# A third weights buffer, hats asked for in every pass, products spread over two passes, and smaller buffers elsewhere, in a deformable-convolution block

## The chip, the cores and the metric

One NeuronCore of a Trainium2 chip runs the whole program. The metric is device time in microseconds (us) of one execution. Executions of one kernel lie within about 0.5% of each other. Every kernel was timed in rounds with the kernel before on the same chip. A ratio is the mean time of one kernel's fast runs over that of the kernel before's fast runs of the same rounds, so it is not quite the ratio of the medians that are quoted; it comes with a 95% interval.

## The reference, cut to what matters

The input is (2, 256, 128, 128) in f32. Layer 0 normalises it, then runs three branches of deformable depthwise convolution with dilations 1, 9 and 12; each branch samples 9 taps at positions moved by learned offsets, with bilinear weights:

```python
py = yy - pad + ky * dil + off[:, :, 0]
px = xx - pad + kx * dil + off[:, :, 1]
sampled = _bilinear(x, py, px)              # four neighbours, weight (1-|dy|)(1-|dx|)
y = einsum('bckhw,ck->bchw', sampled, wk)   # 9 taps, per channel
x_i = gelu(ln2d(y))
# out = ln2d(x1 + x2 + x3 + conv1x1(x)); h = mlp(out); x = x + ln2d(h + out)
```

Layer 1 is a 3x3 convolution with ternary weights. The change does not touch it.

## The kernel before

There are three stages: A makes the normalised image as a table in DRAM and, for every tap, *hats*, the one-dimensional weights max(0, 1-|offset - r|) (negated) for rows and for columns; B samples; C is layer 1. The change is in B.

B works in units: one image, one row of tiles (3 rows high), one branch. A tile `xs` is a patch of 9 x 14 pixels (126 partitions) by 256 channels; 17 tiles make a row of tiles, and all three branches use them. For a unit, the matrix `A` (126 x 3456) holds the bilinear weights. It is the product of the column hats, which are loaded straight into `A`, and the row hats `hy`, which VectorE multiplies in, one product for each `ky` (three a unit inside the image). TensorE multiplies every tile by its part of `A` into PSUM (`pm`), ScalarE copies `pm` to `ev`, and VectorE adds the taps of `ev` into a ring of output rows (the *sums*). A unit has two passes, one for each half of the channels. Between these matmuls a *tail* is woven in, one step at a time: norms, GELU, the 1x1 convolution and the MLP of finished rows.

```python
def load_columns(u):                 # SyncE's queue, straight into A
    for ky in taps(u):
        src, at, n = hat_rows(u, ky, TR, [[HY * 3 * W, TC], [0, TR]])
        pin(nc.sync.dma_start(k["A"][u % 2][0:PT, AO + at : AO + at + n], src))

def load_rows():                     # ScalarE's queue, into one of HBUFS = 3 tiles
    if ahead and len(hys) < HBUFS:
        ...
        pin(nc.scalar.dma_start(hy[0:PT, 0:n], src))

def build():                         # the product
    hy, u, at, n = hys.popleft()
    A = k["A"][u % 2][0:PT, AO + at : AO + at + n]
    pin(nc.vector.tensor_tensor(A, A, hy[0:PT, 0:n], ALU.mult))

def sample(u, c):                    # one pass
    for T in range(0, NT, 2):
        # two tiles: matmuls into pm, one copy pm -> ev; in the last pass of a row also
        # load_tile(next row, T + XAHEAD); XAHEAD = 4
        for _ in range(-(-len(pending) * 2 // (NT + 1 - T))):
            pending.popleft()()      # sums of the pass before, products
        if c == 0 and T == 0:
            for _ in range(HBUFS): load_rows()
        tail.advance()
    ...                              # cut: the first XAHEAD tiles of the next row
    if kys: pending.extend(sums(u, c, ev))
    if c == KC - 1:
        if u + 2 < len(units): load_columns(u + 2)
        pending.append(lambda: complete(u))
    elif u + 1 < len(units):
        pending.extendleft([build] * len(taps(u + 1)))   # all products of u+1 first
```

`pin` keeps the emitted order, so the order in which these calls are made is the order on every engine.

## Time and profile before

| | kernel before |
|---|---|
| median of the first 3 runs | 8623.69 us (8601.57 to 8631.41) |
| profiled span | 8590.6 us |
| first to last pm matmul | 957 to 7303 us, 264 units, 24.04 us each |
| granted TensorE clock in that stage (share of full speed) | 0.91 |
| VectorE idle in front of the products | 1061.8 us |
| ScalarE waiting for the sums to free `ev` | 869.3 us |

The group line of the products shows how such a line is read: line, engine, operation, names, shapes, count; then busy us and mean ns of one; then the idle time in front of them with what ended it.

```profile
L727 DVE TENSOR_TENSOR A<-A,hy 126x1152 f32<-126x1152 f32 (+2 forms) x752 | 1000.7, 1344 | 1061.8 <-DMA hy<-hats 618.6 <-DMA A<-hats 361.9 <-PE pm L826 39.7
```

VectorE stands as long before the 752 products as it works on them. Both factors come late: the row hats (618.6 us) and the columns (361.9 us).

### The profile page before, as it was taken

How to read it: one execution, taken by the hardware profiler on the slowest of the kernel's cores; microseconds unless marked ns; L12 is line 12 of the kernel's file. 1: busy time of each engine (PE TensorE's matmuls, PEld its weight loads, DVE VectorE, ACT ScalarE, POOL GpSimd, SP SyncE). 2: the span in 40 equal slices, each digit the busy share in tenths (PEclk: the TensorE clock that was granted, in tenths of full speed). 3: DMA queues.
4: the chain of work that ended last, by engine and by line, in shares of the span. 5: the costliest groups of instructions: out<-in, count | busy, mean ns of one | idle time of the engine just before them, and what ended most of it. 6: DMA issues, size and time to landing. Idle time of an engine off the chain costs nothing. (4 is left out here: it accounts for less than half of the span.)

```text
span 8590.6 us, 100764 instructions
## 1 busy us (share of the span) xinstructions
PE 7303.7 (85%) x33648; PEld 5392.7 (63%) x33648; DVE 6012.3 (70%) x11183; ACT 4362.5 (51%) x8530; POOL 1160.6 (14%) x1740
## 2 busy tenths in 40 slices
PE   6999778888888888888887888888888888789999
PEld 3555576766666766776666766766766766334444
DVE  7666467777767777776667777767777776387676
ACT  2444345655555655555655655555655556433232
POOL 0000001211211211112211111211221112200000
PEclk9999788999899989999989998999999999799999
DMA  8777566666666666665566666666666665212121
GB/s 298 197 192 197 171 200 209 213 195 213 206 191 201 211 200 201 217 204 185 187 190 211 217 200 215 204 196 199 217 203 192 217 206 174 86 69 77 66 78 53
DMA packets 776262, 1579.90 MB, mean 184 GB/s; under 512 B 96496, under 2 KB 492232, under 8 KB 771376
## 3 DMA queue, kind: packets, MB, share of 16 engines
q1 hardware_dynamic: 588528, 872.06, 32.9%
q10 hardware_dynamic: 122688, 466.35, 16.6%
q0 software_dynamic: 64512, 234.91, 8.2%
q8 instruction: 270, 4.42, 0.2%
q14 instruction: 264, 2.16, 0.1%
HBM read 1306.71 MB, written 266.36 MB: 183 GB/s over the span
## 5 line engine op out<-in xcount | busy, mean ns | idle before, releaser
L826 PE MATMUL pm<-A,xs 126*128 126x216 f32 (+2 forms) x17952 | 3828.1, 363 | 710.5 <-ACT ev L835 466.3
L826 PEld LDWEIGHTS pm<-A,xs 126*128 126x128 f32 x17952 | 3380.8, 206 | 1183.9 <-ACT ev L835 585.0
L835 ACT COPY ev<-pm 128x432 f32<-128x432 f32 (+2 forms) x4752 | 2202.8, 490 | 2124.0 <-PE pm L826 964.9
L778 DVE SCALAR_TENSOR_TENSOR ring<-ev,defw,ring 128x384 f32<-128x384 f32 (+5 forms) x4376 | 2380.9, 566 | 119.6 <-ACT ev L835 27.5
L727 DVE TENSOR_TENSOR A<-A,hy 126x1152 f32<-126x1152 f32 (+2 forms) x752 | 1000.7, 1344 | 1061.8 <-DMA hy<-hats 618.6
L502 ACT ACTIVATE T<-T,rs 128x256 f32<-128x256 f32 x1280 | 703.5, 606 | 45.3 <-DMA hy<-hats 30.0
L771 DVE TENSOR_SCALAR ring<-ev,defw 128x384 f32<-128x384 f32 (+2 forms) x568 | 308.3, 550 | 471.3 <-ACT ev L835 470.7
L453 PE MATMUL hp<-T,w 128*128 128x512 f32 x1024 | 530.0, 642 | 121.1 <-ACT T L597 116.0
L493 POOL TENSOR_SCALAR rs<-mv 128x4 f32<-128x4 f32 x320 | 181.2, 566 | 3035.5 <-DVE mv L491 2813.8
L1159 PE MATMUL pc<-cring,signs 128*128 128x512 bf16 x2304 | 519.8, 384 | 57.2 <-DVE signs L1047 42.7
L517 PE MATMUL zc<-ident,T 128*128 128x128 f32 x2560 | 405.5, 296 | 169.2 <-DVE T L656 77.1
L1159 PE MATMUL pc<-cring,sums 128*128 128x512 bf16 x2304 | 510.3, 380 | 0.0
L453 PE MATMUL h<-hT,w 128*128 128x512 f32 x1024 | 480.0, 592 | 0.9 <-ACT hT L612 0.9
L517 PEld LDWEIGHTS zc<-ident,T 128*128 128x128 f32 x2560 | 329.5, 152 | 227.1 <-ACT T L502 89.0
L204 PE MATMUL pz<-wz,xa 128*128 128x486 f32 x1024 | 460.5, 582 | 1.5 <-DVE zr L211 1.5
L489 DVE BATCH_NORM_STATS2 st<-T 128x6 f32<-128x256 f32 x1280 | 447.8, 411 | 13.7 <-ACT T L479 13.4
L479 ACT COPY T<-tp 128x512 f32<-128x512 f32 x640 | 384.0, 602 | 144.5 <-DMA hy<-hats 47.5
L1159 PEld LDWEIGHTS <-signs 128*128 128x128 bf16 x2304 | 226.6, 99 | 339.6 <-issue 42.1
L1159 PEld LDWEIGHTS <-sums 128*128 128x128 bf16 x2304 | 225.4, 98 | 274.4 <-DVE sums L1219 0.2
L453 PEld LDWEIGHTS hp<-T,w 128*128 128x128 f32 x1024 | 196.6, 202 | 289.3 <-ACT T L597 167.7
L495 POOL TENSOR_TENSOR rs<-rs,mhalf 128x4 f32<-128x4 f32 x320 | 375.4, 1173 | 0.0
L540 ACT ACTIVATE T<-zc,bb,bw 128x512 f32<-128x512 f32 x384 | 304.0, 794 | 107.1 <-DMA hy<-hats 46.5
(124 smaller groups left out, 6163.7 us busy)
## 6 DMA issues: line engine op xcount, KB each, us to landing
hy<-hats ACTq DMA_DIRECT2D x736, 567.0 KB
A<-hats SPq DMA_DIRECT2D x736, 567.0 KB
xs<-table SPq DMA_DIRECT2D x1496, 126.0 KB
g12d<-T POOLq DMA_DIRECT2D x128, 512.0 KB, 4.9
other<-g12d POOLq DMA_DIRECT2D x128, 512.0 KB, 5.3
hats<-hb SPq DMA_DIRECT2D x192, 240.0 KB
hats<-hb SPq DMA_DIRECT2D x192, 192.0 KB
xl<-x1d SPq DMA_DIRECT2D x56, 640.0 KB
```

The costliest lines, as they stand in the source:

```text
L204: nc.tensor.matmul(pz[:, 0:NZ], lhsT=xt[:, c, r, :], rhs=k["wz"][:, c, :], start=c == 0, stop=c == KC - 1,)
L453: nc.tensor.matmul(out, lhsT=w, rhs=v, start=start and i == 0, stop=stop and i == n - 1)
L479: nc.scalar.copy(Tv[:, 2 * h : 2 * h + 2, :].rearrange("p j c -> p (j c)"), tp)
L489: pin(nc.vector.bn_stats(st[:, j, :], Tv[:, j, :]))
L495: pin(nc.gpsimd.tensor_tensor(rs[:, 0, :], rs[:, 0, :], mhalf[:, 0:NB4], ALU.pow))
L502: nc.scalar.activation(Tv[:, j, :], Tv[:, j, :], AF.Identity, scale=rs[:, 0, j : j + 1], bias=rs[:, 1, j : j + 1],)
L517: nc.tensor.transpose(zc[:, j * P : (j + 1) * P], Tv[:, j, c * P : (c + 1) * P], ident)
L727: pin(nc.vector.tensor_tensor(A, A, hy[0:PT, 0:n], ALU.mult))
L778: nc.vector.scalar_tensor_tensor(dst, src, w, dst, ALU.mult, ALU.add)
L826: nc.tensor.matmul(pm[:, j, 0:n], lhsT=xts[b, Rt][T + j][0:PT, c * P : (c + 1) * P], rhs=rhs, start=True, stop=True,)
L835: nc.scalar.copy(ev[:, q0 * 3 : q1 * 3, T * CI : (T + nt) * CI].rearrange("p m (t j) -> p t m j", j=CI), pm[:, 0:nt, 0:n].rearrange("p t ( ...
L1159: nc.tensor.matmul(pc[:, bank, :], lhsT=w[:, m * P : (m + 1) * P], rhs=xc[:, i, k, t * JC : (t + 1) * JC, kx : kx + W], start=j == 0, stop ...
```

## The change

The intent is to take the products off the critical path: a third `A`, so that products are made ahead of their use, and products spread over both passes instead of standing in a block at the head of one. On-chip memory for the third `A` (13.9 KB a partition) is found by cutting other buffers. One more row of tiles covers the last image rows when the rows are no multiple of three.

```diff
-NORMS = 4
-VBUFS = 9
-HBUFS = 3
-XAHEAD = 4
+NORMS = 3
+VBUFS = 8
+HBUFS = 2
+ABUFS = 3
...
-    NR = (H + 2 * REACH) // RI
+    NR = -(-(H + 2 * REACH) // RI)
...
             while self.norms == NORMS:
-                yield 1, None, 1
+                yield 0                      # and advance() goes on to the next chain
...
-            xt = pool.tile([P, C], F32, name="xs", tag="xs", bufs=NT + XAHEAD)
+            xt = pool.tile([P, C], F32, name="xs", tag="xs", bufs=NT)
...
-                if c == 0 and T == 0:
-                    for _ in range(HBUFS):
-                        load_rows()
+                if T == 0:
+                    load_rows()              # now fills up to HBUFS, ahead of the pops
...
-            if c == KC - 1:
-                if u + 2 < len(units):
-                    load_columns(u + 2)
-                pending.append(lambda: complete(u))
-            elif u + 1 < len(units):
-                pending.extendleft([build] * len(taps(u + 1)))
+            n = [len(taps(v)) if v < len(units) else 0 for v in (u + 2, u + 3)]
+            if c == 0:
+                for i in range(n[0] - 1):
+                    pending.insert(1 + len(pending) * i // 2, build)
+            else:
+                if n[1]:
+                    load_columns(u + 3)
+                    pending.append(build)
+                pending.append(lambda: complete(u))
```

More of the change, by code (lines that the diff above doesn't have):

```diff
@@ L426, in advance @@
                     step = next(item[1], None)
+                    if step == 0:
+                        continue
                     if step is None:
@@ L711, in load_columns @@
                 src, at, n = hat_rows(u, ky, TR, [[HY * 3 * W, TC], [0, TR]])
-                pin(nc.sync.dma_start(k["A"][u % 2][0:PT, AO + at : AO + at + n], src))
+                pin(nc.sync.dma_start(k["A"][u % ABUFS][0:PT, AO + at : AO + at + n], src))
         def load_rows():
-            if ahead and len(hys) < HBUFS:
+            while ahead and len(hys) < HBUFS:
                 u, ky = ahead.popleft()
@@ L725, in build @@
             hy, u, at, n = hys.popleft()
-            A = k["A"][u % 2][0:PT, AO + at : AO + at + n]
+            A = k["A"][u % ABUFS][0:PT, AO + at : AO + at + n]
             pin(nc.vector.tensor_tensor(A, A, hy[0:PT, 0:n], ALU.mult))
@@ L806, in sample @@
             if kys:
-                A = k["A"][u % 2]
+                A = k["A"][u % ABUFS]
                 q0, q1 = (kys[0] + 1) * RI, (kys[-1] + 2) * RI
@@ L843, in sample @@
                     for i in range(T, T + nt):
-                        if i + XAHEAD < NT:
-                            load_tile(*following, i + XAHEAD)
+                        load_tile(*following, i)
+                if T == 0:
+                    load_rows()
                 for _ in range(-(-len(pending) * 2 // (NT + 1 - T))):
                     pending.popleft()()
-                if c == 0 and T == 0:
-                    for _ in range(HBUFS):
-                        load_rows()
                 tail.advance()
@@ L854, in sample @@
                 pending.popleft()()
-            if br == BRS[-1] and c == 0 and u + 1 < len(units):
-                for T in range(XAHEAD):
-                    load_tile(*units[u + 1][0:2], T)
             if kys:
                 pending.extend(sums(u, c, ev))
-            if c == KC - 1:
-                if u + 2 < len(units):
-                    load_columns(u + 2)
+            n = [len(taps(v)) if v < len(units) else 0 for v in (u + 2, u + 3)]
[6 more added lines that the diff above has]
+                    pending.append(build)
                 pending.append(lambda: complete(u))
-            elif u + 1 < len(units):
-                pending.extendleft([build] * len(taps(u + 1)))
         pending = deque()
@@ L870, in sample_near @@
         ahead = deque((u, ky) for u in range(len(units)) for ky in taps(u))
-        for u in range(2):
+        for u in range(ABUFS):
             load_columns(u)
-        for _ in taps(0):
-            load_rows()
-            build()
-        for _ in range(HBUFS):
-            load_rows()
+        for u in range(ABUFS - 1):
+            for _ in taps(u):
+                load_rows()
+                build()
+        load_rows()
+        if taps(ABUFS - 1):
+            pending.append(build)
         for u in range(len(units)):
@@ L986, in conv_preact_kernel @@
             k = {
-                "A": [pool.tile([P, AO + 9 * RI * W + AE], F32, name=f"A{i}") for i in range(2)],
+                "A": [pool.tile([P, AO + 9 * RI * W + AE], F32, name=f"A{i}") for i in range(ABUFS)],
             }
```

## The prediction

> **What bounds the kernel now.** I read the page first, then the busy time by stage, the list of waits, and last the order in time of one stretch. The page says that no engine is full, that TensorE comes nearest, and that its clock is below full in the long middle part only.
>
> ```profile
> PE 7303.7 (85%) x33648; PEld 5392.7 (63%) x33648; DVE 6012.3 (70%) x11183; ACT 4362.5 (51%) x8530; POOL 1160.6 (14%) x1740
> ...
> PEclk9999788999899989999989998999999999799999
> DMA  8777566666666666665566666666666665212121
> ```
>
> The sampling stage runs from the first pm matmul (957 us) to the last (7303 us). The change touches nothing else but an order here and there. The windows give, after the stretch: busy us of PE, PEld, DVE, ACT, POOL, then granted clock, DMA share, GB/s.
>
> ```profile
> 0.00:957.00 957.00, 832.64 (x3401) 466.41 (x3401) 622.61 (x1345) 346.73 (x641) 3.44 (x9) 0.97 0.75 217
> 957.00:7303.00 6346.00, 5307.23 (x25157) 4392.56 (x25158) 4538.74 (x8705) 3599.54 (x7524) 1106.28 (x1635) 0.91 0.63 202
> 7303.00:7600.00 297.00, 200.14 (x662) 99.64 (x662) 151.78 (x345) 124.84 (x189) 50.18 (x95) 0.78 0.23 79
> 7600.00:8590.00 990.00, 963.71 (x4432) 434.11 (x4430) 699.17 (x790) 291.43 (x177) 0.74 (x1) 0.99 0.19 69
> ```
>
> The stage has 2 images x 44 rows of tiles x 3 branches = 264 units, so 6346/264 = 24.04 us a unit, in two passes (one per half of the channels). The waits inside the stage (us in total, times, longest):
>
> ```profile
> ACT ev L835 <- DVE ring L778: 869.3, 169, 12.4
> DVE A L727 <- DMA hy<-hats: 618.6, 303, 8.0
> DVE ring L771 <- ACT ev L835: 470.7, 113, 11.3
> DVE A L727 <- DMA A<-hats: 349.2, 126, 14.7
> ...
> PE pm L826 <- ACT ev L835: 466.3, 250, 6.0
> PE pm L826 <- DVE A L727: 197.2, 57, 29.3
> ```
>
> Read from the bottom: PE waits for ACT to empty pm; ACT waits because the ev buffer it wants (two of them) has not been summed by VectorE; VectorE is late because, ahead of the sums, it stands at the products A = A*hy (L727), whose two factors are still in flight. One instance, VectorE then TensorE:
>
> ```profile
> 3076.20 1.36 DVE L727 TENSOR_TENSOR A<-A,hy 126x1152 f32<-126x1152 f32 x1 [6.19 <-DMA hy<-hats]
> 3078.91 1.36 DVE L727 TENSOR_TENSOR A<-A,hy 126x1152 f32<-126x1152 f32 x1 [1.35 <-DMA hy<-hats]
> 3081.48 1.36 DVE L727 TENSOR_TENSOR A<-A,hy 126x1152 f32<-126x1152 f32 x1 [1.21 <-DMA hy<-hats]
> 3089.00 0.61 DVE L771 TENSOR_SCALAR ring<-ev,defw 128x384 f32<-128x384 f32 x1 [6.16 <-ACT ev L835]
> ```
> ```profile
> 3072.31 3.66 PE L453 MATMUL hp<-T,w 128*128 128x512 f32 x4 [7.16 <-ACT T L597]
> 3075.80 0.90 PE L826 MATMUL pm<-A,xs 126*128 126x216 f32 x4
> 3076.53 1.88 PE L453 MATMUL hp<-T,w 128*128 128x512 f32 x4
> ```
>
> The same four matmuls take 3.66 us just after the 7.16 us gap and 1.88 us four microseconds later: a gap is paid twice, as idle time and as slow matmuls.
>
> **What the Trainium skill says.** The page "TensorE: Matmul & The Clock Gate", Part 1 (the HAM clock gate), says that the array falls to half clock after about 3.4 us of idleness and needs about as long of activity to come back; the trace agrees (granted clock 0.54 from 3072.3 to 3076.0 us, 1.00 after). The same page, under the architectural detail, says ScalarE and VectorE take their queues strictly in order: so a product that waits for a transfer holds up every sum behind it, as above. "DMA: Bandwidth & Descriptors", section "Issuing engines are not separate DMA queues", says transfers started from several engines share the same 16 DMA engines: so asking for hats on ScalarE's queue and columns on SyncE's at once makes both late. "Perfetto Trace Analysis", section "Identifying the Most-Contended Engine", says that a repeating bubble on the engine that should be full can mean too few buffers; here the repeating bubble is at L727 and the A buffers are two.
>
> **What the floors are.** TensorE at full clock: 34 pm matmuls of 216 columns took 6.37 us together (0.187 each); by columns 15640 x 0.187 + 1904 x 0.125 + 408 x 0.062 = 3190 us. The 2360 wide tail matmuls in the stage start 0.43 us apart (3076.53 to 3078.25 for four), 1015 us; the 4848 transposes 0.11 apart, 530 us. Sum 4735 us or 17.9 us a unit. The stage is then 4735 of warm work, 5307 - 4735 = 572 lost to the clock (9% of 6346 is 571), and 6346 - 5307 = 1039 idle. VectorE: 4539/264 = 17.2 us a unit. DMA: 202 GB/s x 6346 us/264 = 4.86 MB a unit; its bursts run at 255 to 290 GB/s, so about 18 us. Three resources of nearly one size, chained by small buffers: none can be filled wholly.
>
> **The change part by part.**
>
> Balance. VectorE's sums are (2378 + 308)/528 = 5.1 us a pass, the three products 1000/264 = 3.8 us a unit, the tail's share 853/528 = 1.6 us a pass. Before, all three products open pass 1: 10.5 us of work there, against 6.7 in pass 0 and 9.0 us of TensorE per pass. So pass 1 is VectorE's even with no wait, and with two ev buffers it cannot lend to pass 0. After, one product closes pass 0 and two lie in pass 1: 8.0 and 9.2 us. That alone is worth at most 10.5 - 9.2 = 1.3 us a unit.
>
> Transfers. Before, at a unit's start three columns and three hats (6 x 0.567 MB) plus the tail's 0.45 MB, nearly 3.9 MB, or 14 us at 270 GB/s, are wanted at the front of pass 1, some 12 us later. VectorE's idle time in front of L727 is 1049 us in all, 4.0 us a unit. After, with a third A, the columns are for the unit three ahead, the first product comes at the end of the next pass, the third in the middle of the one after, and one hat is asked for a pass later. 2.8 MB (10.5 us) are wanted over 11 to 16 us. I expect about three quarters of those 4.0 us to go, and the 197 us of PE waiting straight for A.
>
> What is taken away to pay for it: hats buffers 3 to 2, tail tiles 9 to 8, norms 4 to 3, tiles read ahead 4 to 0. I counted the emitted order: there is no point, before or after, where the sums must push the tail to free a ring; waiting chains average 0.38 before and 0.36 after. So the smaller tail costs nothing in the steady state. The rows of the image that are now read only in the last pass still have a pass to land.
>
> The extra row. Six more units: two are empty, four have one tap (72 columns). Eight passes of 34 narrow matmuls, nine copies of about 0.35 us and a few sums: about 4 us each, +32 us. But they carry tail work: the emitted drain after the last sample shrinks from 277 steps to 231. It took about 200 us, so 46 x 0.72 = -33 us. One more unit prepared at the start: +8 us. About +10 in sum, nothing much.
>
> Sum. TensorE's side: of 24.04 - 17.9 = 6.1 us of idle and slow time a unit I keep 60%, 3.7, since gaps shorten and the clock recovers with them: 21.6. VectorE's side, as a check: 17.2 work + 1.0 left at L727 + the 2.9 of other waits it has now = 21.1. I take the worse: 264 x (24.04 - 21.6) = 644 us gained, 10 lost: 8624 - 634 = 7990. I round up to 8010, for coupling I can't see.
>
> **The rivals.**
>
> (a) The hats become the wait. With two buffers the third hat can't be asked for until the unit's first product is done, at the end of pass 0, and it is ScalarE that stands at the issue, in order, with the pm copies behind it. If the first product waits for its columns, ScalarE stops and TensorE soon after; and the third product follows the issue by only some 5 to 8 us. For it: a hat took long to land in bursts (the 6.19 us above), and ScalarE already shows small waits of this kind (99.5 us before ev). Against it: at that point in pass 1 only tile rows load, and in every third unit alone. If so, half the gain: 8300.
>
> (b) The DMA engines bind at 18 us a unit: waits at L727 stay because supply, not timing, is short. For it: share 0.85 to 0.97 in bursts. Against: whole 5 us stretches near 3085 and 3118 us show under 40 GB/s, so there is room. 8200.
>
> (c) It goes better: TensorE stays warm through the stage and the unit comes to 20.3 us: 7650. Against it: a third of PE's waits is at the tail's matmuls (T, xn), which the change leaves.
>
> (d) No gain, because the copies of ScalarE and the two ev buffers pace it in any case: ACT has 13.6 us a unit of work, so it could not on its own. 8550.
>
> **Range and chances.** A unit between 20.8 and 22.9 us gives 7790 to 8340; I take 7790 to 8370. Everything removed lies on the chain that stops TensorE, and what is added cancels, so faster by over 2% (under 8451) is 0.90, within 2% 0.08, slower 0.02.
>
> **What would show it.** Right: idle time before the products well under 1049 us, say 250 to 450; ACT's wait for the sums of 869 us under half; no PE wait for A; stage clock 0.94 or more; about 21.6 us a unit over 264 full-size units; stages before and after unchanged. Wrong: a large wait of VectorE or ScalarE for hy (rival a), or DMA share near 0.8 with L727 still waiting (rival b).

## The result, and the profile after

The changed kernel takes 8502.81 us (median of 4, 8491.07 to 8530.18) against 8614.66 us of the kernel before in the same rounds: ratio 0.9874, interval 0.9843 to 0.9905. It is 1.3% faster, where 7% was predicted. The prediction was wrong.

The page of the changed kernel:

```profile
PE 7301.8 (86%) x33920; PEld 5371.4 (63%) x33920; DVE 5994.7 (71%) x11212; ACT 4358.4 (51%) x8602; POOL 1144.7 (13%) x1740
...
PEclk9999789999999999999899999999999999899999
DMA  9777667666666666665567666766666665212121
```

The stretches of the sampling stage and of the drain behind it (after: two lines; then the drain of the kernel before):

```profile
947.00:7254.00 6307.00, 5352.75 (x25539) 4396.13 (x25539) 4530.66 (x8774) 3619.30 (x7636) 1101.40 (x1656) 0.92 0.66 205
7254.00:7394.00 140.00, 111.23 (x368) 57.70 (x366) 56.00 (x149) 76.47 (x134) 37.59 (x73) 0.89 0.21 68
```
```profile
7303.00:7499.00 196.00, 152.73 (x477) 80.19 (x476) 68.82 (x191) 99.64 (x174) 48.85 (x93) 0.82 0.20 67
```

The sampling stage lost only 39 us (6346 to 6307) and its clock went from 0.91 to 0.92. More than half of the gain of the profiled runs (8590.6 - 8489.2 = 101 us) is in the drain, from the last pm matmul to the last statistics of the tail, 196 to 140 us. The waits inside the stage (us in total, times, longest):

```profile
DVE A L729 <- DMA hy<-hats: 555.3, 240, 7.6
DVE A L729 <- DMA A<-hats: 424.0, 121, 11.8
ACT ev L837 <- DVE ring L780: 589.2, 180, 8.5
ACT ev L837 <- DVE ring L773: 168.4, 55, 7.2
PE pm L828 <- ACT ev L837: 523.3, 308, 6.6
PE pm L828 <- DMA xs<-table: 152.8, 127, 4.8
PE pm L828 <- DVE A L729: 27.8, 1, 27.8
```
```profile
PE pm L826 <- DMA xs<-table: 24.8, 15, 5.2
```

The last line is of the kernel before. TensorE no longer waits for `A` (197.2 us before; the 27.8 us left are one wait at the start), which is what a third buffer is for. But the products still wait for both factors, 979 us against 968 before, and a new wait has appeared: TensorE for its tiles, 152.8 us against 24.8. ScalarE's wait for the sums stands in two lines now, 757.6 us together, against 869.3 in one line before.

One instance in order of time, from the queues of SyncE and ScalarE and from VectorE:

```profile
3004.38 2.53 SPq L714 DMA_DIRECT2D A<-hats  x3
```
```profile
3008.84 1.68 ACTq L722 DMA_DIRECT2D hy<-hats  x2
```
```profile
3019.05 1.36 DVE L729 TENSOR_TENSOR A<-A,hy 126x1152 f32<-126x1152 f32 x1 [5.00 <-DMA hy<-hats]
```

The columns are asked for at the end of a unit, the hats at the head of the next pass, and the product stands at the end of that pass. So everything lies within one pass, as it did before the change. The product is for a unit that will need it only two units later, and yet VectorE stands 5.00 us for it, with the sums behind it.

### The profile page after: what moved, and what is told of

It reads as the page before. It is cut to its first block, busy times and chain, and to the rows that moved or that the text cites. A ratio compares the mean times of both kernels' runs of the same rounds, so it can differ in the third digit from the quotient of the medians.

```text
span 8489.2 us, 101867 instructions
## 1 busy us (share of the span) xinstructions
PE 7301.8 (86%) x33920; PEld 5371.4 (63%) x33920; DVE 5994.7 (71%) x11212; ACT 4358.4 (51%) x8602; POOL 1144.7 (13%) x1740
## 5 line engine op out<-in xcount | busy, mean ns | idle before, releaser
L828 PE MATMUL pm<-A,xs 126*128 126x216 f32 (+2 forms) x18224 | 3861.7, 360 | 708.9 <-ACT ev L837 523.3
L837 ACT COPY ev<-pm 128x432 f32<-128x432 f32 (+3 forms) x4824 | 2203.8, 488 | 2139.4 <-PE pm L828 1113.3
L729 DVE TENSOR_TENSOR A<-A,hy 126x1152 f32<-126x1152 f32 (+2 forms) x756 | 1015.9, 1344 | 1143.0 <-DMA hy<-hats 555.3
L1146 ACT CAST cring<-D 128x2048 bf16<-128x2048 f32 x128 | 243.3, 1901 | 223.5 <-PE pc L1162 152.7
```

The lines of the kernel that those rows point to most:

```text
L828: nc.tensor.matmul(pm[:, j, 0:n], lhsT=xts[b, Rt][T + j][0:PT, c * P : (c + 1) * P], rhs=rhs, start=True, stop=True,)
L837: nc.scalar.copy(ev[:, q0 * 3 : q1 * 3, T * CI : (T + nt) * CI].rearrange("p m (t j) -> p t m j", j=CI), pm[:, 0:nt, 0:n].rearrange("p t ( ...
```

## The experiments

Three theories stood at first. *L, the lead*: the third buffer's time went between product and use, not between fetch and product. *S, the supply*: the DMA engines cannot deliver faster. *C, the coupling*: the waits of the products are not what a unit's time hangs on.

### e1_late: products one pass later

```diff
             if c == 0:
-                for i in range(n[0] - 1): pending.insert(1 + len(pending) * i // 2, build)
+                if n[0]: pending.append(build)
             else:
-                if n[1]: load_columns(u + 3); pending.append(build)
+                for i in range(n[0] - 1): pending.insert(1 + len(pending) * i // 2, build)
+                if n[1]: load_columns(u + 3)
```

> The changed kernel with each unit's first product moved one pass later and the other two likewise: columns now have two passes from the request to the first product instead of one. Theory L (the third buffer's time went between product and use, not between fetch and product, so the lead of the fetch stayed one pass): VectorE's idle time in front of the products falls from 1143 us to 300 to 500 us, ScalarE's wait for the sums (589 + 168 us) to under 400, time 8200 to 8350 us. Theory S (the DMA engines' supply): idle time moves to the hats, stays over 800 us, time within 0.5% of the change, 8460 to 8540. Theory C (the products' waits are not what the unit's time hangs on): the idle time falls but the time stays within 0.5%.

Measured: 8624.43 us, ratio 1.0006 (0.9979 to 1.0034). It is slower than the change.

```profile
L729 DVE TENSOR_TENSOR A<-A,hy 126x1152 f32<-126x1152 f32 (+2 forms) x756 | 1014.6, 1342 | 1024.2 <-DMA hy<-hats 953.6 <-DMA xs<-table 26.8 <-PE pm L828 16.2
```

The columns' wait is gone from the first three releasers, as L says, but nearly all of it has moved to the hats, 953.6 us. With two hats buffers and three products a unit, the third hat can be asked for only when the first product is done, at the head of the pass in which it is used; and in this version the new columns are asked for at just that time. So L alone falls, and S is not shown either. This is theory H.

### e2_no_columns and e2_no_hats: take the transfers away

Their outputs are wrong, which doesn't matter for the times.

```diff
-            for ky in taps(u):
+            for ky in taps(u) if u < ABUFS else ():       # both: columns of the first units only
...
-            pin(nc.vector.tensor_tensor(A, A, hy[0:PT, 0:n], ALU.mult))
+            pin(nc.vector.tensor_tensor(A, hy[0:PT, 0:n], hy[0:PT, 0:n], ALU.mult))
...                                                        # e2_no_hats: two hats loaded once, kept
```

> Wrong result on purpose: no column loads after the first three units, product = hat times hat. 1.7 of 4.9 MB a unit and every wait for columns are gone. Theory L and theory S both: VectorE's idle time at the products under 400 us and the time 8000 to 8250 us. Theory C: 8400 or more.

> Wrong result on purpose: neither columns nor hats are loaded after the start, product = a kept hat times itself; the products stay. 3.4 of 4.9 MB a unit are gone, no product waits for a transfer. It is the ceiling of what any fetch order could bring. By the prediction's step (products' waits are worth most of 4.0 us a unit): a unit of about 21.6 us, 7850 to 8000 us. Theory C: 8300 us or more, because TensorE, ScalarE and VectorE wait for each other anyway.

Measured: without columns 8150.95 us, ratio 0.9457 (0.9432 to 0.9482); without columns and hats 7687.57 us, ratio 0.8921 (0.8899 to 0.8943). The sampling stage of the second:

```profile
964.00:6467.00 5503.00, 5062.42 (x25538) 4211.75 (x25538) 4493.71 (x8774) 3639.40 (x7636) 1146.84 (x1656) 0.97 0.25 77
```

With the same instructions on VectorE and no product waiting, the stage takes 5503 us, or 20.8 us for each of 264 full units, at clock 0.97. The run also takes the traffic off everything else, so it is a ceiling, and what the waits alone are worth is not shown by it; for that see e6, which keeps the traffic. In e2_no_columns the hats' wait is 283.8 us instead of 555.3, with the hats asked for at the same places: without the columns they come earlier, in part perhaps because the first product, which frees a hats buffer, no longer waits for its columns.

### e3_row and e4_tail: the small parts alone, on the kernel before

```diff
-    NR = (H + 2 * REACH) // RI
+    NR = -(-(H + 2 * REACH) // RI)               # e3_row
```
```diff
-NORMS = 4                                         # e4_tail
-VBUFS = 9
+NORMS = 3
+VBUFS = 8                                         # and yield 0 with its two lines in advance()
```

> The kernel before with nothing but the extra row of tiles. The prediction: +32 us of narrow passes, -33 us of drain, so within 20 us of the kernel before (8600 to 8635). A rival: the row costs 60 us or more and eats the gain of the other parts, 8670 or more.

> The kernel before with nothing but the smaller tail (8 tiles, 3 norms, a chain that waits for a norm no longer takes the step). The prediction: no cost in the steady state, so within 0.4% of the kernel before, 8580 to 8640. Rival: the tail's order is worth part of the 1.3% gained: under 8560.

Measured: e3_row 8617.12 us, ratio 1.0008 (0.9973 to 1.0043); e4_tail 8628.53 us, ratio 1.0012 (0.9980 to 1.0043). On the kernel before neither costs or gains anything that shows.

### e5_hats3 and e6_late_hats3: three hats buffers

```diff
-HBUFS = 2
+HBUFS = 3
-VBUFS = 8
+VBUFS = 7        # room; two constants are moved out of the stage as well
                  # e6: and the products one pass later, as in e1_late
```

> The changed kernel with three hats buffers again (room: tail tiles 8 to 7, and two constants moved out of the stage). Theory H (with two hats buffers each unit's third hat can be asked for only at the start of the pass that uses it, behind the columns): the hats part of VectorE's idle time at the products (555 us) falls under 250, the columns part (424 us) stays, time 8300 to 8420. Theory S (supply of the DMA engines): the sum of both parts stays over 850 us and the time within 0.5% of the change.

> Later products and three hats buffers together: columns have two passes, every hat at least one. Theory H plus L: idle time at the products under 300 us in all (after: 1143, later products alone: 1003), the unit near 22.5 us, time 7950 to 8200. Theory S: idle time over 700 us, 8400 or more. Either alone is known or runs beside it; if this gains more than the sum of the two, each hides the other.

Measured: e5 8433.80 us, ratio 0.9790 (0.9754 to 0.9826); e6 8199.28 us, ratio 0.9510 (0.9478 to 0.9541). Their products, e5 then e6:

```profile
L733 DVE TENSOR_TENSOR A<-A,hy 126x1152 f32<-126x1152 f32 (+2 forms) x756 | 1014.1, 1341 | 751.8 <-DMA A<-hats 609.7 <-DMA hy<-hats 70.1 <-PE pm L832 49.6
```
```profile
L733 DVE TENSOR_TENSOR A<-A,hy 126x1152 f32<-126x1152 f32 (+2 forms) x756 | 1012.4, 1339 | 33.6 <-DMA A<-hats 15.5 <-issue 11.4 <-DMA hy<-hats 6.4
```

Three hats alone take the hats' wait from 555 to 70 us, and the columns' wait grows to 610. Three hats and later products together leave 33.6 us of 1143. So S falls for the waits at the products: the same bytes arrive in time when they are asked for early enough. H and L are both true, and each hides the other. With two hats, later products cost 1.3% (1.0006/0.9874); with three they gain 2.9% (0.9510/0.9790 = 0.9714). With the waits goes time, so C falls too, in its strict form.

The tail of seven tiles needs a control, on the change:

> The change with seven tail tiles instead of eight and nothing else: control for e5, e6, e12. The emitted order has no forced step and a drain of 263 steps instead of 231, so within 0.5% of the change, 8480 to 8550.

Measured: e9_tail7 (only `VBUFS = 7`) 8558.86 us, ratio 0.9958 (0.9924 to 0.9993). That is 0.9% slower than the change, a little more than expected: e5 and e6 gained in spite of their tail, and their true distance from the change is larger by about that much. Against this control e6 is 4.5% faster (0.9510/0.9958), for 1135 us less of waits at the products (1168.4 in e9). That is some 385 us, so a microsecond of these waits was worth about a third of a microsecond of time (an estimate; e6 has other waits that e9 has not).

### e8_spread: the spreading alone, with two A buffers

```diff
 # on the kernel before; A, hats, tail, read-ahead untouched
-            if c == KC - 1:
-                if u + 2 < len(units): load_columns(u + 2)
-                pending.append(lambda: complete(u))
-            elif u + 1 < len(units):
-                pending.extendleft([build] * len(taps(u + 1)))
+            n = [len(taps(v)) if v < len(units) else 0 for v in (u + 1, u + 2)]
+            if c == 0:
+                for i in range(n[0] - 1): pending.insert(1 + len(pending) * i // 2, build)
+            else:
+                if n[1]: load_columns(u + 2); pending.append(build)
+                pending.append(lambda: complete(u))
 # and the hats asked for at the head of every pass, as in the change
```

> The kernel before (two A buffers, three hats, larger tail) with nothing but the products spread over the passes as in the change. The lead of the columns is then the same as in the change. Theory L/H: the third A buffer bought nothing, so this is as fast as the change or a little faster, 8400 to 8530. Rival: the third buffer is what gained the 1.3%, and this stays at 8600 or, with PE waiting for A, is slower.

Measured: 8157.07 us, ratio 0.9464 (0.9433 to 0.9496). This part alone is four times as good as the whole change, and far better than I expected.

```profile
L727 DVE TENSOR_TENSOR A<-A,hy 126x1152 f32<-126x1152 f32 (+2 forms) x752 | 1008.8, 1341 | 482.0 <-DMA A<-hats 380.7 <-DMA hy<-hats 70.5 <-PE pm L826 29.9
...
ACT ev L835 <- DVE ring L778: 509.5, 171, 8.8
ACT ev L835 <- DVE ring L771: 74.7, 37, 5.2
```

Products that are spread wait 482 us instead of 1062, and ScalarE waits 584 us for the sums (two lines) instead of 869.3. No third buffer was needed. (With the products the requests for hats have moved, to the head of every pass; no run separates the two.) So the question turned round: what did the rest of the change take away?

### e10, e11, e14: the cuts, put back onto e8 one by one

```diff
-XAHEAD = 4        # e10_spread_noahead, e14_spread_both_cut
+XAHEAD = 0
-HBUFS = 3         # e11_spread_hats2, e14_spread_both_cut
+HBUFS = 2
```

> The fast e8_spread (two A buffers, three hats, products spread) with the read-ahead of tiles taken away (4 to 0), as the change did. Theory X: SyncE issues a tile every 0.88 us, so 17 of them take 15 us, longer than the pass they are squeezed into, and the columns queue behind them; then the time goes from 8157 to 8380 to 8460, and PE's waits for tiles from 52 us to over 150. Rival: the read-ahead is worth under 0.7%, 8140 to 8215.

> e8_spread with two hats buffers instead of three. Theory H: hats become the wait again (70 us now, 400 or more then), 8230 to 8350. If both cuts add up to what the change lost (8503 - 8157 = 346 us), the third A buffer is worth nothing by itself.

> e8_spread with both cuts of the change at once: two hats buffers and no read-ahead, still two A buffers. If the third A buffer is worth nothing by itself: 8440 to 8520, as the change (8503). If it gains: 8560 or more here. If it costs (its columns, earlier, crowd the hats): 8430 or less.

Measured: e10 8351.33 us, ratio 0.9707 (0.9691 to 0.9723); e11 8272.51 us, ratio 0.9618 (0.9602 to 0.9634); e14 8415.20 us, ratio 0.9785 (0.9751 to 0.9819). The waits, e10, then e11, then e14:

```profile
DVE A L727 <- DMA A<-hats: 578.7, 144, 13.2
...
PE pm L826 <- DMA xs<-table: 168.5, 132, 4.6
```
```profile
DVE A L727 <- DMA hy<-hats: 669.0, 263, 8.3
```
```profile
L727 DVE TENSOR_TENSOR A<-A,hy 126x1152 f32<-126x1152 f32 (+2 forms) x752 | 1010.2, 1343 | 1102.6 <-DMA hy<-hats 539.4 <-DMA A<-hats 468.5 <-PE pm L826 44.9
...
ACT ev L835 <- DVE ring L778: 533.3, 173, 7.8
ACT ev L835 <- DVE ring L771: 176.6, 57, 7.3
```

Without the read-ahead TensorE waits 168.5 us for tiles (52.3 in e8) and the columns come later too, 578.7 us against 380.7. With two hats the hats' wait is back, 669 us against 70.5. Each wait is the one that the changed kernel shows. e14 is also worth a look for what it keeps: its products wait as long as those of the kernel before (1103 against 1062 us), and yet it is 2.2% faster. TensorE waits 197.1 us for `A`, as before, and longer for its tiles (148.5 us). What is left is that the products stand in other places: ScalarE waits 710 us for the sums (two lines) instead of 869.

### e12_ahead4: the change with one cut undone

```diff
+XAHEAD = 4        # tiles read ahead again, as in the kernel before
-VBUFS = 8
+VBUFS = 7         # room
```

> The changed kernel (third A, two hats) with four tiles read ahead again (room: tail tiles 8 to 7). Theory X: 8230 to 8380 instead of 8503. Rival: within 0.7% of the change.

Measured: 8476.04 us, ratio 0.9852 (0.9835 to 0.9868). Against its control with seven tail tiles (0.9958) that is 1.1% faster; against the change it looks like nothing.

```profile
DVE A L730 <- DMA hy<-hats: 800.5, 336, 9.5
...
DVE A L730 <- DMA A<-hats: 157.9, 47, 9.6
```

The columns' wait falls to 158 us and the hats' grows to 800. As with e1 and e5: what one fetch gains, the next one in the line loses, until all of them are early.

### e13_late_hats3_queues: is it the issue of the tiles?

Theory X of the expectations: SyncE's issuing is what makes the tiles late. Without read-ahead, SyncE issues the 17 tiles in a row, and the columns behind them (the changed kernel):

```profile
3027.51 15.17 SPq L688 DMA_DIRECT2D xs<-table  x17
3042.77 2.53 SPq L714 DMA_DIRECT2D A<-hats  x3
```

That is 0.89 us a tile and 15 us in all; one issue takes 0.79 us (median), the rest is waiting. e13 is e6 with every second tile issued from GpSimd's queue:

```diff
-            pin(nc.sync.dma_start(xt[0:PT], src))
+            pin((nc.gpsimd if T % 2 else nc.sync).dma_start(xt[0:PT], src))
```

> e6_late_hats3 (8199 us; third A, later products, three hats, no read-ahead) with every second tile issued from GpSimd's queue instead of SyncE's. Theory X: the 17 issues take half as long, the last pass of a row (15.1 us of the 23.1 us mean unit times three, the longest of the six) comes down to 11 to 12 us, time 7950 to 8080, faster than all others. Rival: it is the transfers and not their issue that fill that pass, or GpSimd's queue stands in the tail's way: within 0.7% of 8199 or slower.

Measured: 8208.80 us, ratio 0.9540 (0.9525 to 0.9556), no faster than e6 (0.9510).

```profile
PE pm L832 <- DMA xs<-table: 225.0, 133, 8.4
SPq L692 <- PE pm L832: 1475.5, 643, 41.7
```

TensorE waits longer for tiles than in e6 (102.0 us), not less. So sharing the issue out between two queues does not help. The last line gives a reason: SyncE's tile requests stand 1475.5 us for pm matmuls, and GpSimd's 1339.4 us (waiting for the pass to begin is in both). With 17 tile buffers for 17 tiles, a tile of the next row can only be asked for when the last pass has used the buffer. That tiles must be asked for earlier is shown by e10 and, against its control, by e12; what share issue and transfer have in the lateness stays open.

### e19, e15, e17, e18: the third buffer itself, and the best version

e19 is the change with `k["A"][u % 2]` instead of three buffers, every request and product in the same place, and nothing else but the start-up before the first unit. e18 is e8 with the extra row. e15 is e8 with the row, the change's tail and its room spent on `XAHEAD = 8`. e17 is e6 with `XAHEAD = 4`, for which the tail has to go down to six tiles.

> The change with two A buffers instead of three; same places of every request and product, same hats, tiles, tail and row. If the third A costs: 8400 to 8450, as e14. If the tail and the row are what made e14 faster: 8480 to 8530 as the change. If it gains: 8560 or more.

> e8_spread with the extra row (which by e3 costs nothing alone): 8140 to 8190, 3.5% or more faster than the change and as complete in what it samples.

> Two A buffers, products spread, three hats buffers, the smaller tail and the extra row of the change, and its 4 KB spent on tiles read ahead (8 instead of 4). Read-ahead from 0 to 4 was worth 194 us; from 4 to 8 I expect 0 to 80 more, so 8070 to 8170: faster than the kernel before, the change and e6. Rival: it saturates or the earlier tiles crowd the columns, 8170 to 8250.

> Third A, later products, three hats, four tiles read ahead, which fits only with six tail tiles (the emitted order then has 223 steps forced by a full ring, 4.6%). If a third A buffer with all fetches on time is worth something: no waits at the products, PE's waits for tiles under 60 us, time 8000 to 8130 in spite of the tail. If the tail of six costs more than that: 8200 or more, and it stays open.

| kernel | median us | ratio | 95% interval |
|---|---|---|---|
| e19_change_two_a | 8468.85 | 0.9826 | 0.9807 to 0.9845 |
| e18_spread_row | 8208.32 | 0.9534 | 0.9517 to 0.9551 |
| e15_spread_row_ahead8 | 8185.66 | 0.9517 | 0.9478 to 0.9556 |
| e17_late_hats3_ahead4 | 8252.59 | 0.9603 | 0.9568 to 0.9638 |

TensorE's waits in e19; the change has 27.8 and 523.3 us in their place:

```profile
PE pm L828 <- DVE A L729: 227.5, 87, 25.3
PE pm L828 <- ACT ev L837: 343.5, 286, 6.6
```

With two buffers the change is no slower than with three, rather 0.5% faster, with intervals that just touch. (e14 had come out in its range for a third buffer that costs. The 8469 us of e19 lie between its ranges for "costs" and for "the same".) The third buffer takes away 200 us of waiting for `A`, and TensorE waits 180 us longer for ScalarE to empty pm. So it gains nothing in this place; whether it costs a little is not settled. The extra row costs 0.7% on e8 (0.9534/0.9464), more than I expected, though it cost nothing that shows on the kernel before. A read-ahead of eight is not clearly better than four. e17 does not settle what a third buffer with all fetches early could bring, since its tail of six has 223 forced steps; that stays open for want of on-chip memory. Still, its trace is worth knowing: its products wait only 43.0 us and TensorE only 20.6 us for tiles, and yet e8, with 482 and 52 us, is 1.5% faster. Fetches that are on time may not be enough when the tail pays for them.

Both e15 and e18 give the correct result, cover the extra row, and beat the kernel before by 4.7 to 4.8% and the change by over 3%. The fastest correct kernel is e8, 5.4% ahead of the kernel before, without the row. On this data all are correct.

## Why the prediction was wrong

All ratios are to the kernel before. The way from there to the change, in steps that each differ by one thing or one pair:

| step | kernel | ratio |
|---|---|---|
| products spread, hats asked for in every pass | e8_spread | 0.9464 |
| hats 3 to 2 and read-ahead 4 to 0 | e14_spread_both_cut | 0.9785 |
| smaller tail and the extra row | e19_change_two_a | 0.9826 |
| third A buffer | the change | 0.9874 |

The first two steps are clear of noise. The intervals of the third overlap, and those of the last just touch.

**What bounds the kernel.** Right in kind: without the waits at the products the kernel is faster (e6). The size is not shown to be right. With no waits and no hats' traffic the time is 7688 us (e2_no_hats), close to the 7650 of rival (c), but e6, which has hardly a wait at the products and keeps the traffic, stands at 8199, above the predicted 7990; part of that may be its smaller tail and its late tiles. The sum "I keep 60%" gave a unit of 21.6 us; the change has 23.9 (6307/264). Two readings were wrong. The bursts are not bounded by 290 GB/s: 5 us stretches of the same trace show 310, 322 and 353, so 18 us a unit is no floor for DMA (13.8 at 353, an estimate). And the 6.19 us under rival (a) is VectorE's idle time, not the time that a hat took to land.

**Balance.** The runs speak for it: in e14 the products wait as long as before, and the time is 2.15% less, 185 of 8592 us or 0.7 us a unit, under the "at most 1.3", although e14 also pays for late tiles. But e14 moves the waits together with the products, so that it is the balance that gains is argued, not shown.

**Transfers: the step that failed.** "I expect about three quarters of those 4.0 us to go." They did not: 1062 us became 1143. The prediction itself put the columns' request and the first product one pass apart, as they were before. What was to help was that 2.8 MB are wanted over 11 to 16 us, instead of nearly 3.9 MB in some 12, since "one hat is asked for a pass later". (The 2.8 leave out the tail's 0.45 MB that the 3.9 contain.) That took a delay for a relief. With two hats buffers the hat that is asked for late is itself the wait: 669 us in e11, against 70.5 in e8. And without the read-ahead the columns stand in SyncE's queue behind 17 tiles: 578.7 us in e10, against 380.7. The spreading did bring a good part of what was expected, 1062 to 482 us in e8, with two `A` buffers. The third `A` lengthens only the way from product to use. TensorE's 197 us of waiting for `A` went, as predicted, but came back as waiting for ScalarE (e19). Time for the fetch comes from moving the product away from its request (e6), and that needs the hats to be early too.

**"What is taken away to pay for it."** This is the same failure, seen from the cuts, which were counted as free. The sentence on the tiles, that they "still have a pass to land", was wrong: the cut alone costs 2.6% (e10 against e8, 0.9707/0.9464). And rival (a), hats as the wait, to which I gave half the gain (8300), is the second cut, 1.6% alone (e11 against e8); both together cost 3.4% (0.9785/0.9464). So what was left of the spreading's 5.4% after the payments was 1.3%. For the tail the prediction looked at the emitted order and wrote that it costs nothing. From nine tiles to eight that holds on the kernel before (e4), and in the changed order it was not tested alone; one tile fewer still, a cut that the change does not make, costs 0.9% there (e9). The rival's mechanism is not quite as I put it either: ScalarE stops less at its requests for hats than before (the profile's sum of what waited behind them on ScalarE is 48 us, against 256 before); it is VectorE that waits, for the hat that was asked for late.

**The extra row.** "About +10 in sum": not contradicted on the kernel before (e3, 1.0008, interval 0.9973 to 1.0043). In the faster e8 it costs 0.7%. The drain shrank by 56 us where 33 was written, and is most of what the profiled run gained.

**Rival (b), supply.** Refused for the products' waits by e6, which moves the same bytes and leaves 33.6 us of waits. Traffic is not without effect: without the columns the hats' wait halves (e2_no_columns). And e6 is 6.6% above e2_no_hats (0.9510/0.8921), and what of that the traffic costs in other places is not settled.

## What to carry to other kernels

Another buffer helps only what lies between its filling and its emptying: before you buy one, mark on the time line where the request, the arrival, the use and the release are, and ask which of these distances grows. If it is paid for with other buffers, test the cuts one by one, since a fetch that becomes late can eat the gain of the one that became early, and undoing one of several such cuts can show nothing until the others are undone too. And spreading a block of work that holds up a queue over the passes may bring the gain without any memory, as e8 did.

## What the Trainium skill lacked or had wrong

- "Perfetto Trace Analysis", Optimization Strategy: a repeating bubble on the engine that should be saturated can mean that there is no room for the next tile. That sentence leaves open which buffer is short. Here the bubble stood on VectorE (70% busy, TensorE 85%), in front of the products. One more buffer for their result left it at 1143 us (1062 before), one more for the hats at 751.8 (e5), later products alone at 1024.2 (e1), the last two together at 33.6 (e6).
- "DMA: Bandwidth & Descriptors", Issuing engines are not separate DMA queues: the time to start a transfer is called usually small beside the transfer. For one tile that holds: its issue takes 0.79 us on SyncE and 0.60 on GpSimd (medians), and from GpSimd's issue to the landing it is 6.6 us (median, e13). What this section leaves out is that issues add up in a queue while transfers overlap: 17 tiles are 13.4 us of issue, more than the 12 us of an average pass (24 us a unit). It says that a second issuing engine saves the time of issue only. In e13 SyncE issues 9 tiles of a row instead of 17, and nothing is gained (0.9540 against 0.9510); both queues stand for pm matmuls, 1475.5 and 1339.4 us.
